# The opening of a four-layer kernel: wider filler products for TensorE, gated loads, another order of the first loads

## The chip, the cores and the metric

The program runs on one core of one Trainium2 chip. A core has a matrix engine (TensorE, "PE" in the profile; its weight loads are "PEld"), three engines for elementwise work (VectorE "DVE", ScalarE "ACT", GpSimd "POOL") and SyncE ("SP"), which here only issues DMAs. The metric is the device time of one execution in microseconds (us). Before the change the median of three runs is 757.54 us, with the runs between 756.88 and 757.93.

## What is computed

`x` has 64 sequences of 64 tokens with 256 features (4096 tokens), and `cond` has one vector of 64 numbers for each sequence. Four layers follow each other:

```python
# layer 0: conditioned RMS norm, GELU-gated FFN, 8-bit activations and ternary weights in the down product
scale = cond @ norm_w.T + 1.0
h = x * (scale[:, None, :] * rsqrt(mean(x * x) + 1e-6))
val, gate = split(h @ up_w.T)                     # 2 x 1024
x = act_quant(val * gelu(gate)) @ weight_quant(down_w).T + x
# layer 1: conditioned RMS norm, attention with 16 heads in each sequence; norm, SwiGLU FFN (1024)
x = x + a_alpha * attention(norm(x)) ; x = x + f_alpha * swiglu(norm(x))
# layer 2: layer norm plus tanh(cond @ lin_w.T + lin_b)
# layer 3: adapter whose two matrices are made from cond for each sequence
Wd_b = Wd + 0.1 * (cond @ Wdd.T + bdd) ; Wu_b = Wu + 0.1 * (cond @ Wdu.T + bdu)
x = x + relu(x @ Wd_b + bd) @ Wu_b + bu
```

The arrays are fp32. The large products take each operand as a high and a low part in a 32-bit matmul format and add up three products of the parts (high-high, high-low, low-high).

## The kernel before

The tokens are worked on in 8 blocks of 512, each block in 4 tiles of 128. Layer 0 is one loop over the 32 tiles (`l0`, with n the tile's number); the change lies in its opening, before tile 2, and in three loads that the loop issues.

**A tile of layer 0.** `upper(n, ch)` makes, for each of two halves `ch` of the 1024 gate and value columns, 12 products of 512 columns into one PSUM bank for the gate and 12 into one for the value (`mm3`, L83 to L85; for tiles 0 and 1 `first`, L423). ScalarE applies GELU to the gate bank (L441), VectorE multiplies with the value bank (L442). `quant(n)` on VectorE rounds the result to whole numbers (L448 to L453), and a transposing DMA on SP turns it round (L455). `lower(n)`, some three tiles later, makes the down product (L467), and VectorE scales it and adds x (L468). The eight PSUM banks go round among all of these. At set tiles ("visits", first n = 5, 9 and 12) four generator blocks for layer 3 are made as well (`gen_make`, L289; `gen_stage`, L304; `gen_store`, L311, which is a DMA issued by POOL).

**Splitting weights.** Weights arrive in fp32 in a staging tile; ScalarE makes the high part by a copy (`half_hi`, L332), VectorE the low part by a subtraction (`half_lo`, L336). The same is done for x times its scale (`prep_parts`, L401 to L406; for the first half block at L497 to L500). For the weights of attention this is the class `Splitter`: `load` (L195) brings one 128x256 piece to one of two staging buffers, `turn` (L201, L202) splits the oldest piece that is there and loads another. The loop calls `load` at tile 7 and `turn` at tiles 8 to 15.

**Who sets the order.** On PE, ACT, DVE and POOL the order is that of the program text. SP's order is that of the text in the opening alone; after it a planner puts SP's DMAs in the order in which it expects them to be able to go, so that a load whose buffer is free early can go out far ahead of its place in the text. Three loads do: the two first pieces of the attention weights (`st`), and block 2's x (`xt`). Where the program must hold a load back, GpSimd writes one column of its target first, reading something that is ready only at the wanted time: the load then has to wait for that write (L278 for the generator's weights, L378 for block 1's x, L387 for `upst3`).

**The opening.** SP issues `condT` (L105), the two chunks of the first half block of x in feature-major form (L374), then `upst3`, x's first block in token-major form (`xt0`, L389), `upst1`, the rest of x's block (L391) and `condT` again (L392). ACT issues the norm's weights (`cwn`, L106) and the four pieces of `upst2` and `upst0` (L328). TensorE meanwhile runs six filler products (`warm`, L477) of a zeroed tile `idle`, the scale's products (`cond_vector`, L121), and five filler products more. Then `first((0, 1), 0)` and `first((0, 1), 1)` make the 48 products of tiles 0 and 1, in the order up2, up0, up3, up1 of the weights. Block 0's sums of squares (`prep_scale`, L223) stand on ACT between the split of up3 and that of up1.

Of the kernel before, what the change touches and what calls it, by code (L numbers as in the profile page):

```python
# [8 lines left out]
F32 = mybir.dt.float32  # L9
F32R = mybir.dt.float32r  # L10
BF16 = mybir.dt.bfloat16
# [6 lines left out]
P = 128  # L18
# [4 lines left out]
T = 512  # L23
# [13 lines left out]
def tile_kernel(ctx: ExitStack, tc, xT, x, condT, cw, upT, downT, qkvT, woT, ghT, outT_w,  # L37
                vecs, rows, g1, g2, gb, out):
    nc = tc.nc

    const = ctx.enter_context(tc.tile_pool(name="const", bufs=1))
# [10 lines left out]
    pools = {}  # L52
# [9 lines left out]
    def bank(tag):  # L62
        uid[0] += 1
        tags = pools["tags"]
        if tag not in tags:
            tag = "mm"
        return pools["ps"].tile([P, 512], F32, tag=tag, bufs=tags[tag], name=f"{tag}_{uid[0]}")
# [6 lines left out]
    def block(name):  # L74
        return main.tile([P, TT, D], F32, tag="x1", bufs=X1, name=name)

    def tok(ap, i):

        return ap[i * T:(i + 1) * T, :].rearrange("(t p) d -> p t d", p=P)
# [16 lines left out]

    ident = const.tile([P, P], F32, name="ident")
    make_identity(nc, ident)
    idle = const.tile([P, P], F32, name="idle")
    nhalf = const.tile([P, TT], F32, name="nhalf")  # L100
    nc.vector.memset(idle, 0.0)
    nc.gpsimd.memset(nhalf, -0.5)
    ct = const.tile([P, NB], F32, name="ct")
    cwn = main.tile([64, D], F32, tag="st", bufs=2, name="cwn")
    nc.sync.dma_start(out=ct[0:64], in_=condT)  # L105
    nc.scalar.dma_start(out=cwn, in_=cw[:, V_NORM, :])  # L106

    gl = pools["a"].tile([P, NB], F32, name="gl")
# [72 lines left out]
    class Splitter:  # L181
# [5 lines left out]
                         for hi, lo, src, kc, n, step in jobs for c in range(kc) for j in range(0, n, step)]  # L187
            self.there = []

        def load(self):  # L190
            if self.todo:
                hi, lo, v, c, js = self.todo.pop(0)
                uid[0] += 1
                st = main.tile([P, 512], F32, tag="st", bufs=2, name=f"st{uid[0]}")[:, :js.stop - js.start]
                nc.sync.dma_start(out=st, in_=v[:, c, js])  # L195
                self.there.append((hi[:, c, js], lo[:, c, js], st))

        def turn(self):
            if self.there:
                hi, lo, st = self.there.pop(0)  # L200
                nc.scalar.copy(hi, st)  # L201
                self.eng.tensor_tensor(lo, st, hi.bitcast(F32), ALU.subtract)  # L202
            self.load()

    def two(pool, name, kc, n):
        return [pool.tile([P, kc, n], F32R, name=f"{name}{k}") for k in range(2)]
# [19 lines left out]
    def parts(name):  # L226
        return [main.tile([P, 2, T], F32R, tag=k, bufs=2, name=f"{k}{name}") for k in ("xh", "xl")]
# [86 lines left out]
    def l0(hooks):  # L314
# [6 lines left out]
        blk, til = {}, {}  # L321

        ups, xfs = {}, {}

        def load_up(j, queue, chunks=slice(0, 2)):
            if j not in ups:
                ups[j] = main.tile([P, 2, 512], F32, tag="x1", bufs=X1, name=f"upst{j}")
            queue.dma_start(out=ups[j][:, chunks],  # L328
                            in_=upT.rearrange("(c p) n -> p c n", p=P)[:, chunks, j * 512:(j + 1) * 512])
# [35 lines left out]
        def prep_load(i):  # L365
            xf = pool.tile([P, 2, T], F32, tag="xf", bufs=1, name=f"xf{i}")
            xt = None if i == 0 else block(f"xt{i}")
            xfs[i] = xf
            blk[i] = [xt, None, parts(f"l0_{i}"), None]
            src = xT.rearrange("(c p) t -> p c t", p=P)[:, :, i * T:(i + 1) * T]  # L370
            if i == 0:

                for c in range(2):
                    nc.sync.dma_start(out=xf[:, c, :T // 2], in_=src[:, c, :T // 2])  # L374
            else:
                nc.sync.dma_start(out=xf, in_=src)
                if i == 1:
                    nc.gpsimd.tensor_copy(xt[:, 0, 0:1], ups[1][:, 0, 0:1])  # L378
                nc.sync.dma_start(out=xt, in_=tok(x, i))

        def rest_load():
# [91 lines left out]
        def warm(n):  # L473

            pb = bank("mm")
            for _ in range(n):
                nc.tensor.matmul(pb[:, :P], lhsT=idle, rhs=idle, start=True, stop=True)  # L477

        for c in range(2):
            load_up(2, nc.scalar, slice(c, c + 1))  # L480
        prep_load(0)
        til["ones"] = pool.tile([P, P], F32, name="ones")

        nc.scalar.activation(sa, nhalf[:, 0:2], AF.Gelu)
        nc.gpsimd.memset(til["ones"], 1.0)
        for c in range(2):
            load_up(0, nc.scalar, slice(c, c + 1))
        rest_load()
        warm(6)
        half_hi(2, 0)  # L490
        cond_norm()
        warm(5)

        for c in range(2):
# [31 lines left out]
        for n in range(N + 2):  # L526
            if n < N:
                if n > 1:
                    upper(n, 0)
                if n == 0:  # L530
                    ternary_load()
                if n in visits:
                    for _ in range(4):
                        gen_make()
                        gen_stage()
                for _ in range(0 if n == 4 else 2 if n in visits and (n + 3 in visits or n == visits[-1]) else 1):
                    gen_load(ups[1][:, n % 2, n:n + 1] if n < 4 else None)
                    gen_store()
                upper(n, 1, "rest" if n < 2 else None)
                if n == 1:  # L540
                    ternary()
                    blk[0][3] = block("x1_0")
                if n == 4:
                    ternary_rest()
                if n % TT == 0 and n // TT + 1 < NBLK:
                    prep_load(n // TT + 1)
                if n % TT == 1 and n // TT + 1 < NBLK:
                    for _ in prep_parts(n // TT + 1):
                        pass
                if n % TT == 2 and n // TT + 1 < NBLK:  # L550
                    prep_scale(n // TT + 1)
# [443 lines left out]
    nc.gpsimd.memset(vx, 0.0)  # L995
    splits = Splitter(nc.vector, (qkv[0], qkv[1], qkvT, 2, 3 * D, 256), (wo[0], wo[1], woT, 2, D, 256))

    hooks = {2: [cond_load], 7: [splits.load]}
    for n in range(8, 16):
        hooks[n] = [splits.turn]  # L1000
    hooks[10].append(cond_rest)
    last = NBLK * TT
    turned = []
# [11 lines left out]
    hooks[last] = [lambda: a_ahead(0, 5), lambda: turned[0](), lambda: turn_ahead(1), lambda: a_ahead(0, 6), lambda: a_ahead(0, 7)]  # L1015
    hooks[last + 1] = [lambda: turned[1](), lambda: a_begin(2)]
    l0(hooks)
    phase.close()

# [8 lines left out]
    splits = Splitter(nc.gpsimd, (*pools["gh"], ghT, 2, 2 * FF, 512), (*pools["wout"], outT_w, 8, D, 256))  # L1028
# [17 lines left out]
    for w in range(W):  # L1046
        i, tp = divmod(w, 2)
# [87 lines left out]
    for n in range(5, N):  # L1135
        i, f = divmod(n, 8)
# [123 lines left out]
```

## Time and profile before

| | us |
|---|---|
| median of three runs | 757.54 |
| profiled execution | 757.83 |
| its span, first to last instruction | 755.9 |
| PE busy in the span | 744.7 |
| DVE busy | 540.9 |
| ACT busy | 405.8 |
| POOL busy | 340.4 |

Matmuls are pipelined and their ends are modelled, so PE's busy share says little; the distance between the starts of neighbouring matmuls says more. A row of the timeline gives start, duration, engine, line, operation, output and inputs, shapes, the number of instructions that are merged in it and, in brackets, how long the engine had been idle and what ended that. "SPq" and "ACTq" rows are DMA issues. A DMA row gives the queue's engine, the size and the median time from issue to landing.

### The profile page before, as it was taken

How to read it: one execution, taken by the hardware profiler on the slowest of the kernel's cores; microseconds unless marked ns; L12 is line 12 of the kernel's file. 1: busy time of each engine (PE TensorE's matmuls, PEld its weight loads, DVE VectorE, ACT ScalarE, POOL GpSimd, SP SyncE). 2: the span in 40 equal slices, each digit the busy share in tenths (PEclk: the TensorE clock that was granted, in tenths of full speed). 3: DMA queues.
4: the chain of work that ended last, by engine and by line, in shares of the span. 5: the costliest groups of instructions: out<-in, count | busy, mean ns of one | idle time of the engine just before them, and what ended most of it. 6: DMA issues, size and time to landing. Idle time of an engine off the chain costs nothing.

```text
span 755.9 us, 17443 instructions
## 1 busy us (share of the span) xinstructions
PE 744.7 (99%) x7036; PEld 616.5 (82%) x7036; DVE 540.9 (72%) x841; ACT 405.8 (54%) x848; POOL 340.4 (45%) x359
## 2 busy tenths in 40 slices
PE   9999999999999999999999999999999999999997
PEld 7866766776676878888888888888888888888886
DVE  4998878867687688889888866636465555555666
ACT  5553445335435588998889573535253534434242
POOL 2123223123134436766655327464646464545291
PEclk9999999999999999999999999999999999999999
DMA  8897999999995866444665237623261708080821
GB/s 241 253 264 166 270 282 222 296 274 260 223 266 115 186 156 167 113 126 120 160 148 127 80 103 183 140 65 76 72 152 45 179 17 208 1 195 2 229 51 57
DMA packets 117457, 118.88 MB, mean 157 GB/s; under 512 B 39633, under 2 KB 101201, under 8 KB 117377
## 3 DMA queue, kind: packets, MB, share of 16 engines
q1 hardware_dynamic: 109232, 91.29, 49.6%
q0 software_dynamic: 7488, 25.37, 10.8%
q10 hardware_dynamic: 656, 1.11, 0.5%
q8 instruction: 55, 0.90, 0.5%
q14 instruction: 26, 0.20, 0.1%
HBM read 71.41 MB, written 29.56 MB: 134 GB/s over the span
## 4 chain that ended last, share of the span: by engine, by line
PE 84%; DVE 7%; ACT 3%; DMA 3%; issue 2%; POOL 1%; SPq 0%; DVEq 0%; ACTq 0%; POOLq 0%
PE mm L83 10%; PE mm L85 9%; PE mm L84 9%; PE gh L83 7%; PE gh L84 7%; PE gh L85 7%; PE acc L83 4%; PE acc L85 4%; PE acc L84 4%; PE mm L467 4%; PE mm L289 4%; PE S L640 2%; DMA rows<-alphad 2%; PE mm L938 2%; PE mm L681 2%
## 5 line engine op out<-in xcount | busy, mean ns | idle before, releaser
L83 PE MATMUL mm<-up,xhl 128*128 128x512 f32 x240 | 98.0, 408 | 0.0
L83 PE MATMUL gh<-xhf,gh 128*128 128x512 f32 x244 | 97.2, 398 | 0.0
L84 PE MATMUL gh<-xlf,gh 128*128 128x512 f32 x244 | 96.9, 397 | 0.0
L85 PE MATMUL gh<-xhf,gh 128*128 128x512 f32 x244 | 96.9, 397 | 0.0
L787 DVE TENSOR_TENSOR sg<-gh,sg 128x512 f32<-128x512 f32 x61 | 42.0, 688 | 76.0 <-ACT sg L786 39.9
L84 PE MATMUL mm<-up,xhl 128*128 128x512 f32 x240 | 94.8, 395 | 0.0
L85 PE MATMUL mm<-up,xll 128*128 128x512 f32 x240 | 94.8, 395 | 0.0
L441 ACT ACTIVATE g<-mm,rs_l 128x512 f32<-128x512 f32 x64 | 43.8, 689 | 82.7 <-PE mm L85 52.0
L815 DVE TENSOR_TENSOR hlo<-sg,hhi 128x512 fp32r<-128x512 f32 x59 | 56.0, 949 | 31.1 <-ACT hhi L814 30.3
L814 ACT CAST hhi<-sg 128x512 fp32r<-128x512 f32 x59 | 36.5, 619 | 74.2 <-DVE sg L787 73.3
L83 PE MATMUL acc<-wout,hhi 128*128 128x256 f32 x248 | 72.7, 293 | 0.0
L85 PE MATMUL acc<-wout,hlo 128*128 128x256 f32 x248 | 70.3, 283 | 1.1 <-DVE hlo L815 1.1
L442 DVE SCALAR_TENSOR_TENSOR h<-mm,rs_l,g 128x512 f32<-128x512 f32 x64 | 46.5, 744 | 34.6 <-PE mm L85 31.2
L84 PE MATMUL acc<-wout,hhi 128*128 128x256 f32 x248 | 70.1, 282 | 0.0
L251 POOL TENSOR_TENSOR xg<-xg,cv 128x512 f32<-128x512 f32 x32 | 35.3, 1113 | 71.4 <-DVE xg L250 67.3
L83 PEld LDWEIGHTS mm<-up,xhl 128*128 128x128 f32 x240 | 45.1, 188 | 16.2 <-issue 2.4
L85 PEld LDWEIGHTS gh<-xhf,gh 128*128 128x128 f32 x244 | 46.1, 189 | 10.8
L85 PEld LDWEIGHTS mm<-up,xll 128*128 128x128 f32 x240 | 45.0, 188 | 11.0
L84 PEld LDWEIGHTS gh<-xlf,gh 128*128 128x128 f32 x244 | 46.3, 190 | 8.1
L83 PEld LDWEIGHTS gh<-xhf,gh 128*128 128x128 f32 x244 | 46.3, 190 | 8.1
L84 PEld LDWEIGHTS mm<-up,xhl 128*128 128x128 f32 x240 | 45.2, 188 | 9.4
L651 DVE TENSOR_REDUCE mx<-S 128x16 f32<-128x1024 f32 x32 | 39.1, 1221 | 17.3 <-PE S L640 17.3
(215 smaller groups left out, 1928.1 us busy)
## 6 DMA issues: line engine op xcount, KB each, us to landing
gt<-in_g SPq DMA_DIRECT2D x32, 512.0 KB, 9.0
rows<-alphad SPq DMA_DIRECT2D x48, 256.0 KB, 5.1
vb<-vx SPq DMA_DIRECT2D x32, 256.0 KB, 5.3
wd<-s1d SPq DMA_DIRECT2D x32, 256.0 KB, 6.4
wu<-s2d SPq DMA_DIRECT2D x32, 256.0 KB, 6.3
xt<-in_x SPq DMA_DIRECT2D x8, 512.0 KB, 8.4
s1d<-stgs POOLq DMA_DIRECT2D x16, 256.0 KB, 7.3
s1d<-stg POOLq DMA_DIRECT2D x16, 256.0 KB, 7.3
```

The lines of the kernel that those rows point to most:

```text
L83: nc.tensor.matmul(out, lhsT=l[0], rhs=r[0], start=first, stop=False)
L84: nc.tensor.matmul(out, lhsT=l[0], rhs=r[1], start=False, stop=False)
L85: nc.tensor.matmul(out, lhsT=l[1], rhs=r[0], start=False, stop=last)
L251: nc.gpsimd.tensor_tensor(b3(xg), b3(xg), bc(vb, c, i), ALU.add)
L289: nc.tensor.matmul(pb[s][c * 64:(c + 1) * 64], lhsT=gl[h], rhs=gt[h, c * GC:(c + 1) * GC], start=True, stop=True, tile_position=(64 * s, 6 ...
L441: nc.scalar.activation(g, pg, AF.Gelu, scale=rs[:, t:t + 1])
L442: nc.vector.scalar_tensor_tensor(h[:, ch * 512:(ch + 1) * 512], pv, rs[:, t:t + 1], g, ALU.mult, ALU.mult)
L467: nc.tensor.matmul(py[:, :D], lhsT=qt[:, f, :], rhs=wq[:, f, :], start=f == 0, stop=f == 7)
L651: nc.vector.tensor_reduce(ms, sv, AX.X, ALU.max)
L787: nc.vector.tensor_tensor(sg, pv, sg, ALU.mult)
L814: nc.scalar.copy(h_hi, sg)
L815: nc.vector.tensor_tensor(h_lo, sg, h_hi.bitcast(F32), ALU.subtract)
```

## The change

There are three parts.

- The filler. `idle` is a bf16 tile of 128x512 in place of an fp32 tile of 128x128, and each filler product multiplies its first 128 columns with all 512. The counts stay six and five.
- The order of the first loads. On SP the first chunk of x goes first and `condT` second. The second chunk of x goes out on ACT's queue between the two pieces of `upst2`.
- Gates. The first two pieces of the attention weights (the `load` at tile 7 and that in the `turn` at tile 8) are held by a GpSimd write from `gl`, and block 2's x is held by a GpSimd write from `xt0`. GpSimd runs these three writes where they stand in the text: that for block 2's x after the gates of tile 3, the first `st` gate after POOL's store of block 0's result and two generator stores, the second after two generator stores more.

```diff
-    idle = const.tile([P, P], F32, name="idle")
+    idle = pools["a"].tile([P, 512], BF16, name="idle")
...
-    nc.sync.dma_start(out=ct[0:64], in_=condT)
     nc.scalar.dma_start(out=cwn, in_=cw[:, V_NORM, :])
...
-        def load(self):
+        def load(self, held=False):
...
+                if held:
+
+                    nc.gpsimd.tensor_copy(st[:, 0:1], gl[:, 0:1])
                 nc.sync.dma_start(out=st, in_=v[:, c, js])
...
-        def turn(self):
+        def turn(self, held=False):
...
-            self.load()
+            self.load(held)
...
-                for c in range(2):
-                    nc.sync.dma_start(out=xf[:, c, :T // 2], in_=src[:, c, :T // 2])
+                nc.sync.dma_start(out=xf[:, 0, :T // 2], in_=src[:, 0, :T // 2])
+                nc.sync.dma_start(out=ct[0:64], in_=condT)
             else:
                 nc.sync.dma_start(out=xf, in_=src)
-                if i == 1:
-                    nc.gpsimd.tensor_copy(xt[:, 0, 0:1], ups[1][:, 0, 0:1])
+                if i < 3:
+                    nc.gpsimd.tensor_copy(xt[:, 0, 0:1], ups[1][:, 0, 0:1] if i == 1 else blk[0][0][:, 0, 0:1])
                 nc.sync.dma_start(out=xt, in_=tok(x, i))
...
-                nc.tensor.matmul(pb[:, :P], lhsT=idle, rhs=idle, start=True, stop=True)
-
-        for c in range(2):
-            load_up(2, nc.scalar, slice(c, c + 1))
+                nc.tensor.matmul(pb, lhsT=idle[:, :P], rhs=idle, start=True, stop=True)
+
+        load_up(2, nc.scalar, slice(0, 1))
         prep_load(0)
...
+        nc.scalar.dma_start(out=xfs[0][:, 1, :T // 2], in_=xT[P:2 * P, :T // 2])
+        load_up(2, nc.scalar, slice(1, 2))
...
-    hooks = {2: [cond_load], 7: [splits.load]}
+    hooks = {2: [cond_load], 7: [lambda: splits.load(True)]}
     for n in range(8, 16):
-        hooks[n] = [splits.turn]
+        hooks[n] = [lambda n=n: splits.turn(n == 8)]
```

## The prediction

> **What bounds the kernel now.** I read the page's table of engines first (PE 744.7 of 755.9 us busy, so any PE delay goes to the end), then the opening in the timeline, then VectorE's waits, then the timeline where the gated loads are used. Lines of the opening:
>
> ```profile
> 1.05 2.93 PE L477 MATMUL mm<-idle 128*128 128x128 f32 x12 [1.05 <-DVE idle L101]
> ...
> 4.95 2.50 PE L477 MATMUL mm<-idle 128*128 128x128 f32 x10
> ...
> 7.10 2.05 PE L423 MATMUL mm<-up,xhl 128*128 128x512 f32 x4
> ...
> 9.60 1.09 PE L423 MATMUL mm<-up,xhl 128*128 128x512 f32 x4
> ...
> 11.56 0.62 ACT L332 CAST up<-upst 128x512 fp32r<-128x512 f32 x1 [3.13 <-DMA upst<-in_upT]
> ...
> 13.85 0.42 ACT L223 ACTIVATE junkl<-xt 128x256 f32<-128x256 f32 x1 [0.25 <-DMA xt<-in_x]
> ...
> 15.89 1.12 ACT L332 CAST up<-upst 128x512 fp32r<-128x512 f32 x2
> ...
> 16.52 1.29 DVE L336 TENSOR_TENSOR up<-upst,up 128x512 fp32r<-128x512 f32 x2 [2.13 <-ACT up L332]
> ```
>
> Four products take 1.85 us at 7.10 (to the start of the next pair at 8.95), 0.46 each, and 0.93 us at 9.60 (to 10.53), 0.23 each: PE runs at half its rate until about 9.4, though the granted clock in the windows from 0 to 21 us reads 1.00. Then loads bind: ACT waits 3.13 us for up0's second piece, then for xt0 until 13.85; its four squares take 2.04 us, and only then up1 is split, at 15.89. At 16.52 VectorE starts, and its waits in the window from 16.6 to 74 us are, whole:
>
> ```profile
> DVE up L336 <- ACT up L332: 2.1, 1, 2.1
> DVE x L468 <- DVE am L464: 0.2, 1, 0.2
> ```
>
> The first is the wait ending at 16.52. From there VectorE works for 57 us without waiting for another engine. So PE and VectorE are two chains side by side. They meet here (the first row of ACT and of DVE is the use of the first attention piece):
>
> ```profile
> 63.51 0.82 POOL L470 DMA_DIRECT2D x1d<-x  x1 [6.03 <-DVE x L468]
> 64.33 1.23 POOL L311 DMA_DIRECT2D s1d<-stgs  x2
> ...
> 66.89 0.39 ACT L201 CAST qkv<-st 128x256 fp32r<-128x256 f32 x1
> ...
> 69.73 0.42 DVE L202 TENSOR_TENSOR qkv<-st,qkv 128x256 fp32r<-128x256 f32 x1
> 69.99 0.69 ACT L441 ACTIVATE g<-mm,rs_l 128x512 f32<-128x512 f32 x1 [2.71 <-PE mm L85]
> ...
> 73.41 0.48 DVE L468 SCALAR_TENSOR_TENSOR x<-mm,am,xt 128x256 f32<-128x256 f32 x1
> 73.81 0.74 DVE L442 SCALAR_TENSOR_TENSOR h<-mm,rs_l,g 128x512 f32<-128x512 f32 x1
> ```
>
> The generator products at 71.29 (L289) start, group by group, in steps of 0.48, 0.43, 0.43, 0.43, 0.43, 0.47: the seventh group, at 73.95, is 0.04 late. It is the one whose product waits for VectorE by the program's order, and VectorE's L468 ends at 73.89. So at tile 9 VectorE's chain has only that slack: 0.04 us before PE stands. After 74.55 VectorE idles 3.59 us, until 78.15; later delays of it are absorbed.
>
> **The change part by part.**
>
> *Filler.* 22 filler instructions of 0.213 us spacing (5.4 us) become 11. At 0.427 us for 512 columns, the start-to-start time of the products at 7.7 to 8.5, six take 2.6 us and five 2.1 us; at 0.233 us the five take 1.2. The memset (0.17 us for 128 columns) takes 0.17 to 0.68 for 512, and lies before the wait for `condT`. Two cases: PE is at full rate by the first product, or again only near 9.4. With full rate the first product starts when its data is there and the first 18 end about 1.4 us earlier than now; then they wait for up0's second piece, as ACT does already. With half rate the filler ends near 7.7 and the first product is 0.6 us later. Before gave full rate 2.3 us after dense 512-column products began, so I take the first case.
> The Trainium skill ("TensorE: Matmul & The Clock Gate", Part 1) says that the full clock comes after some 3.4 us of sustained activity in a free-running window. By that the new filler, from 1.2 us, would bring it between 4.6 and 8.0, and the rate itself would give 1.4 us. The trace speaks against counting that: it stands ahead of loads that bind.
>
> *First loads.* `condT` is issued one DMA later on SP (xf's rows lie 0.64 us after it, so 1.4 for 0.73); its landing takes 2.8 us, so 4.2 for 3.5; cv and the first scaled x come 0.2 to 0.5 us later (now 5.05 and 5.52). The second chunk of x is issued at about 1.95 for 2.23; VectorE wants it 1.3 us after the first, so the second chunk's splits stay where they are. up2's second piece and up0's pieces go out 0.5 us later on ACT's queue; ACT needs up2's at 6.29 and holds 0.6 us in reserve between up0's second piece and xt0 (three casts of 0.52 from 11.56 reach 13.2, xt0 comes at 13.82). No cost taken.
>
> *Gates.* Three GpSimd writes of 0.18 us, on an engine that idles for 10 us at these places: nothing by themselves. Two effects count.
> (a) The first piece of `st` (128 KB, issued at 2.70 ahead of up3 and xt0) leaves the opening. DMA moves 245 to 363 GB/s there, so xt0 lands about 0.4 us earlier (131 kB at 310). The second piece and block 2's x were issued at 8.58 and 12.94, behind xt0. As squares, up1's split and VectorE's chain follow xt0, the gain is 0.4 us. Bounds: 1.0, if the first load's earlier start (0.64) adds to it; -0.2, if PE stays at half rate until 9.4 (0.6 later, less 0.4 that PE loses now to late splits at 12.96, 13.30, 17.61 and 36.78).
> (b) The first gated `st` now goes out late. On POOL its write stands behind block 0's store, 63.51, and two generator stores, which end at 65.56; so 65.56 + 0.18, issue on SP at 65.80 (SP is free then: the next transpose goes at 67.75). ACT wants the piece at 66.89, VectorE its high part at 69.73. What the load takes is the disputed price. Three rows of the same load, each one DMA in a narrow window:
>
> ```profile
> st<-in_qkvT SPq DMA_DIRECT2D x1, 128.0 KB, 2.3
> ...
> st<-in_qkvT SPq DMA_DIRECT2D x1, 128.0 KB, 4.6
> ...
> st<-in_qkvT SPq DMA_DIRECT2D x1, 128.0 KB, 6.0
> ```
>
> 2.3 at 91.26 with the DMA quiet; 4.6 at 96.62, with block 1's store (95.24) and generator stores just issued by POOL; 6.0 at 71.36, behind a transpose and a 512 KB load on its own queue. At 65.80 POOL has issued block 0's store and generator stores, and DMA is 0.94 to 1.01 busy from 65 to 69: nearest is 4.6. Landing 70.4, ACT's cast 70.45 to 70.85 (ACT stands from 66.99; its GELU moves from 69.99 to 70.9 and is used only at 73.81), VectorE's L202 at 70.9 for 69.73: 1.15 late. All behind it on VectorE is late too, L468 among it, and PE's generator group at 73.95 stands 1.1 us. Bounds: 0 (at 2.3, landing 68.1) and 2.5 (at 6.0, landing 71.8).
> The Trainium skill ("DMA: Bandwidth & Descriptors", Queues, rings and completion order) says that each DMA engine goes round between the queues that have work, a packet at a time. By it a small load on SP's queue would not wait for POOL's stores, would land near the quiet 2.3, and cost nothing: 757.1. The row at 96.62 shows otherwise, 4.6 beside such stores, and decides.
>
> The second gated piece goes out behind the 512 KB load, at 71.3, and is used at 80.66: 9.4 us, free even at 6.0. Block 2's x can go after the transpose at 36.28, so from 37.6; ACT squares it at 53.96: 16 us, against 8.7 for the slowest such load. Later delay of `gt` by it: its fourth tile is used 1.8 us after it lands (40.59), so free.
>
> **Sum.** The later of the two chains counts at 73.95: VectorE's comes at -0.4 + 1.1 = +0.7 us, PE's own would come at -0.4 or, at half rate, +0.2. So +0.7 us. The profiled execution of 757.83 (755.9 span and 1.9 around it) becomes 758.5; it lies 0.3 above the median, so the median goes from 757.54 to 758.2. Nothing gives it back: PE starts its products without gaps from 74.97 on. About 0.2% (1.5 us) is what a measurement of this kernel can tell from no change.
>
> **The rivals.**
> 1. *The gated piece lands in time* (within 3.5 us of its issue): the opening's gain stays, 757.1 (756.5 to 757.6). For it: the load is small and the quiet row 2.3. Against: POOL's stores fill the DMA just then. It would need xt0 a full 1.5 us earlier as well to be told from no change.
> 2. *The gated piece is later than I think* and decides: at 6.0 us VectorE is 2.5 late, sum 2.1, 759.6, slower. It decides from 5.4 us on (5.4 - 3.5 - 0.4 = 1.5). For it: the row at 71.36. Against: nothing stands ahead of it on SP's queue.
> 3. *The filler doesn't do what it says*: half rate until about 9.4 again. Then PE's chain comes 0.2 late by itself. With the piece late that hides behind VectorE's +0.7; with the piece in time the sum is +0.2, 757.7. For it: the wait for `condT` gets longer and falls into the filler. Against: 2.3 us of dense products were enough.
>
> **How the numbers follow.** My forecast 0.52 (757.6 to 759.0), rival 1 0.22, rival 2 0.18, rival 3 with the piece in time 0.08. Range: the lower end takes most of rival 1, 756.6; the upper end goes past rival 2's centre, 759.9, short of the worst bounds together (no gain and 2.5, 760.0). Faster by over 0.2% only if xt0 comes much earlier and the piece in time: 0.09. Slower: rival 2 and the upper tail of the forecast, 0.24. The rest, 0.67, is within 0.2%.
>
> **What would show it.** In the changed kernel: spacing of the first products 0.23 in place of 0.43; `xt` squares at about 13.4 for 13.85, and VectorE's chain from about 16.1; the `st` DMA issued near 65.4 with its time to landing; ACT idle before its first L201 cast until the piece lands, VectorE idle before its first L202 by about 1.1 us, and PE late by as much within the generator products near 73.5. It is wrong if L202 shows no wait there, if PE does not stand when VectorE does, or if the opening moves VectorE's start by more than 1.0 us.

## The result and the profile after

Nine runs of the changed kernel have a median of 759.43 us (758.24 to 760.47); nine of the kernel before, beside them, 757.38 (756.88 to 757.93). The ratio is 1.0028, with a 95% interval of 1.0019 to 1.0037: the change makes the kernel slower by 0.28%, some 2.05 us. The forecast was 758.2 (756.6 to 759.9). The measured time lies inside that range and on the forecast side, but the loss is some 2.05 us where 0.7 was forecast, and 759.43 is outside the 757.6 to 759.0 that the prediction gave to its main case.

The profiled execution took 760.47 us, the slowest of the nine, with a span of 758.4; that of before took 757.83, with 755.9. So the two traces differ by 2.5 us of span. Lines after 95 have moved by up to three (L423 of before is L425, L202 is L204, L468 is L470, L289 is L291).

The opening, from the timeline of the changed kernel (start, duration, engine, line, operation; in brackets the idle time before and what ended it):

```profile
1.17 0.57 SPq L376 DMA_DIRECT2D ct<-in_condT  x1
...
1.18 2.74 PE L479 MATMUL mm<-idle 128*128 128x512 bf16 x6 [1.18 <-DVE idle L101]
...
5.30 1.09 PE L120 MATMUL mm<-ct,cwn 64*128 64x64 f32 x4 [1.38 <-DMA ct<-in_condT]
...
8.07 2.27 PE L425 MATMUL mm<-up,xhl 128*128 128x512 f32 x4
...
12.67 1.09 PE L425 MATMUL mm<-up,xhl 128*128 128x512 f32 x4
...
13.32 0.42 ACT L225 ACTIVATE junkl<-xt 128x256 f32<-128x256 f32 x1
...
16.01 1.29 DVE L338 TENSOR_TENSOR up<-upst,up 128x512 fp32r<-128x512 f32 x2 [1.81 <-ACT up L334]
...
21.07 0.40 PE L83 MATMUL mm<-up,xhl 128*128 128x512 f32 x1
...
21.11 0.75 DVE L444 SCALAR_TENSOR_TENSOR h<-mm,rs_l,g 128x512 f32<-128x512 f32 x1 [1.04 <-PE mm L425]
```

Rows of before to set beside it, those that the prediction does not show:

```profile
3.90 1.11 PE L121 MATMUL mm<-ct,cwn 64*128 64x64 f32 x4
...
19.70 0.40 PE L83 MATMUL mm<-up,xhl 128*128 128x512 f32 x1
...
20.50 0.74 DVE L442 SCALAR_TENSOR_TENSOR h<-mm,rs_l,g 128x512 f32<-128x512 f32 x1
```

The DMA row of `condT`, first before and then changed:

```profile
ct<-in_condT SPq DMA_DIRECT2D x1, 16.0 KB, 2.8
...
ct<-in_condT SPq DMA_DIRECT2D x1, 16.0 KB, 4.0
```

`condT` is issued 0.44 us later than before and needs 4.0 us to land (5.17) instead of 2.8 (3.50). TensorE's six wide products are through by 3.92, so it stands 1.38 us, and its first real product starts at 8.07 for 7.10. Full rate (0.23 us from product to product) comes at 11.74 for 9.37, and the 48 products of the opening end at 21.07 for 19.70: 1.37 us late. The gain on the other chain is there: xt0's squares start at 13.32 for 13.85, VectorE's splits at 16.01 for 16.52, 0.51 us early. The waits of VectorE in the window from 16 to 74 us show where that goes (total, times, longest):

```profile
DVE up L338 <- ACT up L334: 1.8, 1, 1.8
DVE qkv L204 <- ACT qkv L203: 1.3, 1, 1.3
DVE h L444 <- PE mm L425: 1.0, 1, 1.0
DVE x L470 <- DVE am L466: 0.2, 1, 0.2
```

Two rows are new. At 21.11 VectorE waits 1.04 us for the late TensorE, which turns 0.51 early into 0.6 late (21.11 for 20.50); and it waits 1.28 us for the gated piece. That place, tile 9, in the timeline:

```profile
64.08 0.82 POOL L472 DMA_DIRECT2D x1d<-x  x1 [4.59 <-DVE x L470]
...
66.13 0.20 POOL L196 COPY st<-gl 128x1 f32<-128x1 f32 x1
...
66.35 0.33 SPq L197 DMA_DIRECT2D st<-in_qkvT  x1
...
71.23 0.41 ACT L203 CAST qkv<-st 128x256 fp32r<-128x256 f32 x1 [3.04 <-DMA st<-in_qkvT]
...
71.67 0.43 DVE L204 TENSOR_TENSOR qkv<-st,qkv 128x256 fp32r<-128x256 f32 x1 [1.28 <-ACT qkv L203]
...
75.35 0.48 DVE L470 SCALAR_TENSOR_TENSOR x<-mm,am,xt 128x256 f32<-128x256 f32 x1
...
75.89 1.09 PE L291 MATMUL mm<-gt,gl 64*64 64x512 f32 x8 [0.60 <-DVE x L470]
...
76.91 0.50 PE L83 MATMUL mm<-up,xhl 128*128 128x512 f32 x1
```

The gate stands behind POOL's stores, so the load is issued at 66.35; it lands at 71.15, 4.80 us later. ScalarE, VectorE and at last TensorE wait: its seventh generator group at 75.89 comes 1.19 us after the sixth, where a group takes 0.41, so it stands 0.78. VectorE's L470 is at 75.35 for 73.41, and TensorE's first product behind the generators at 76.91 for 74.97: 1.94 us late. From there the shift stays near 1.9 for some 220 us, and VectorE's last instruction is 1.73 us late. The other 0.75 us of the span's 2.5 lies behind that instruction, where SP's last six DMA issues take 3.98 us for 3.25; the second trace of the changed kernel (e9 below) has 1.79 and 0.26 there. The second gated piece and block 2's x, issued late as well, let nobody wait.

### The profile page after: what moved, and what is told of

The parts are those of the page before. It is cut to its first block, busy times and chain, and to the rows that moved or that the text cites. A ratio compares the mean times of both kernels' runs of the same rounds, so it can differ in the third digit from the quotient of the medians.

```text
span 758.4 us, 17430 instructions
## 1 busy us (share of the span) xinstructions
PE 744.5 (98%) x7025; PEld 613.8 (81%) x7025; DVE 541.0 (71%) x841; ACT 406.2 (54%) x848; POOL 342.1 (45%) x362
## 4 chain that ended last, share of the span: by engine, by line
PE 81%; DVE 7%; ACT 5%; DMA 3%; issue 2%; SPq 1%; POOL 1%; DVEq 0%; ACTq 0%; POOLq 0%
PE mm L83 9%; PE mm L85 9%; PE mm L84 9%; PE gh L83 7%; PE gh L84 7%; PE gh L85 7%; PE acc L83 4%; PE acc L85 4%; PE acc L84 4%; PE mm L469 4%; PE mm L291 4%; PE mm L941 2%; PE S L643 2%; DMA rows<-alphad 2%; PE mm L684 2%
## 5 line engine op out<-in xcount | busy, mean ns | idle before, releaser
L789 ACT ACTIVATE sg<-gh 128x512 f32<-128x512 f32 x61 | 35.9, 589 | 29.0 <-PE gh L85 28.4
```

The lines of the kernel that those rows point to most:

```text
L789: nc.scalar.activation(sg, pg, AF.Silu)
```

## The experiments

The theory has two parts. *The gate*: the first gated piece lands too late, and TensorE stands at tile 9. *The first loads*: `condT` is late, TensorE's dense products begin later, and it arrives late at tile 9 by itself. The rival to the first is that the whole loss comes from the opening; the rival to the second, that the order of the loads costs nothing (as predicted) and the wide filler is at fault, or chance. The kernels undo one part of the change or add one part to the kernel before.

This table is read from the profiled execution of each (us from the span's start): the landing of `condT`, the first real product, the start of full rate among the real products, the end of the 48 products of the opening, VectorE's wait before its first split of a piece of `st`, and TensorE's first product behind tile 9's generator products, here "next product". The ratio is that of times to the kernel before beside it, with its 95% interval; it is not simply the quotient of the two medians (for e1 that would be 1.0023).

| kernel | condT | first | full rate | 48 end | wait | next product | ratio |
|---|---|---|---|---|---|---|---|
| before | 3.50 | 7.10 | 9.37 | 19.70 | 0.00 | 74.97 | 1 |
| changed | 5.17 | 8.07 | 11.74 | 21.07 | 1.28 | 76.91 | 1.0028 (1.0019 to 1.0037) |
| changed, again (e9) | 5.08 | 7.99 | 12.11 | 21.21 | 1.17 | 76.92 | 1.0033 (1.0022 to 1.0044) |
| changed without gates on `st` (e1) | 4.33 | 7.23 | 9.66 | 19.68 | 0.00 | 74.69 | 1.0012 (0.9997 to 1.0027) |
| the same again (e10) | 4.54 | 7.03 | 7.37 | 18.47 | 0.00 | 73.47 | 1.0012 (1.0001 to 1.0024) |
| changed, first piece called at tile 4 (e2) | 4.70 | 6.74 | 7.08 | 19.95 | 0.00 | 75.16 | 1.0010 (0.9998 to 1.0023) |
| changed with the old order (e5) | 3.22 | 6.77 | 9.86 | 19.42 | 1.06 | 75.02 | 1.0012 (1.0002 to 1.0022) |
| changed with more filler (e8) | 4.98 | 7.24 | 7.58 | 19.11 | 1.06 | 75.47 | 1.0020 (1.0010 to 1.0030) |
| before plus gates on `st` (e3) | 3.28 | 7.10 | 10.52 | 19.84 | 1.16 | 75.58 | 1.0014 (1.0003 to 1.0025) |
| before plus new order (e4) | 5.34 | 7.38 | 11.13 | 20.23 | 0.00 | 75.25 | 1.0007 (0.9995 to 1.0020) |
| before plus wide filler (e6) | 3.25 | 6.65 | 10.31 | 19.65 | 0.00 | 74.66 | 1.0008 (0.9998 to 1.0018) |
| old order, wide filler, piece at tile 4 (e7) | 3.31 | 6.94 | 8.66 | 18.99 | 0.00 | 74.19 | 1.0002 (0.9993 to 1.0011) |
| before plus gates, piece at tile 4 (e12) | 3.30 | 7.10 | 10.10 | 19.66 | 0.00 | 74.67 | 1.0003 (0.9992 to 1.0014) |
| before plus gates, piece later still (e11) | 3.80 | 7.10 | 9.68 | 19.46 | 5.83 | 81.48 | 1.0121 (1.0103 to 1.0139) |

Single executions scatter: the 28 to 35 runs of before beside the experiments lie between 755.86 and 760.32. Below, one trace shows a mechanism, and the ratio says what it is worth.

### A. The gates on `st` taken out of the changed kernel

```diff
-    hooks = {2: [cond_load], 7: [lambda: splits.load(True)]}
+    hooks = {2: [cond_load], 7: [splits.load]}
     for n in range(8, 16):
-        hooks[n] = [lambda n=n: splits.turn(n == 8)]
+        hooks[n] = [splits.turn]
```

> The changed kernel with the two gates of the attention pieces (st) taken out; filler, new order of the first loads and the gate of block 2's x stay. Late-piece theory: VectorE's 1.28 us wait before its first L204 and the 0.78 us that PE stands in the generator products at 75.9 vanish, so about 1.3 us less than the changed kernel: 758.1. Opening theory (all of the loss comes from the later condT, whose wait on PE grew to 1.38 us, and from PE's half rate until 11.6): the time stays near 759.4. Both expect PE's first half-rate products and the late end of the 48 first products (21.07) to stay.

759.09 us against 757.37, a median 1.7 above, while the ratio, 1.0012 (0.9997 to 1.0027), leaves open whether it is slower at all: its twelve runs reach from 755.47 to 761.03. The trace is clear where the time isn't: no wait at tile 9, groups of generator products in steps of 0.41 and 0.46. So it was run once more, with the changed kernel beside it.

> The changed kernel once more, to have it beside the same runs of the kernel before as the next ones. Both theories: 1.5 to 2.7 us over the kernel before. Trace: VectorE's wait at the first qkv split 1.0 to 1.4 us whatever the opening does; condT at 4.3 to 5.4, full rate anywhere between 7 and 12.

> The first experiment again (the changed kernel without the gates of the attention pieces), beside the changed kernel itself, since its twelve times spread over 5.6 us. Late-piece theory: 0.8 to 1.3 us below the changed kernel of this call. Opening theory: equal to it.

On one chip: changed kernel 759.41 (ratio 1.0033), without the gates 757.92 (1.0012), before 757.14. The gates on `st` cost some 1.5 us in the changed kernel by these medians; e1's ratio makes it 1.2. The same place in the timeline of the kernel without them:

```profile
65.48 0.40 ACT L203 CAST qkv<-st 128x256 fp32r<-128x256 f32 x1
...
68.24 0.42 DVE L204 TENSOR_TENSOR qkv<-st,qkv 128x256 fp32r<-128x256 f32 x1
69.88 0.21 PEld L291 LDWEIGHTS mm<-gt,gl 64*64 64x64 f32 x8 [0.36 <-issue]
69.88 3.66 PE L291 MATMUL mm<-gt,gl 64*64 64x512 f32 x32
```

ScalarE and VectorE show no brackets, and all 32 generator products stand in one row without a gap.

One thing that both theories expected failed: the late end of the 48 products did not stay at 21.07 but came at 19.68 (e1) and 18.47 (e10), with the new order in place. So these two traces differ from that of the changed kernel by more than the wait at tile 9, and the price of the gates is read from the times.

Nor was xt0 later for having the piece in the opening. Its squares start at 13.12 in e1 and here, in e10, at 12.22, for 13.32 (changed) and 13.63 (e9) with the gates:

```profile
12.22 0.42 ACT L225 ACTIVATE junkl<-xt 128x256 f32<-128x256 f32 x1 [0.28 <-DMA xt<-in_x]
```

### B. The gates on `st` alone, in the kernel before

```diff
+                if held:
+                    nc.gpsimd.tensor_copy(st[:, 0:1], gl[:, 0:1])
                 nc.sync.dma_start(out=st, in_=v[:, c, js])
...
-    hooks = {2: [cond_load], 7: [splits.load]}
+    hooks = {2: [cond_load], 7: [lambda: splits.load(True)]}
...
-        hooks[n] = [splits.turn]
+        hooks[n] = [lambda n=n: splits.turn(n == 8)]
```

> The kernel before with the two st gates alone; old filler, old order, block 2's x not gated. Late-piece theory: the opening gains about 0.4 us (xt0 lands near 13.4), VectorE waits 1.2 us at its first qkv split and PE about 0.8 to 1.1 in the generator products: 0.7 over the kernel before, 758.1. Opening theory: the gates cost nothing, 757.0 to 757.4.

758.15 us, ratio 1.0014 (1.0003 to 1.0025): slower by about 1.1 us by the ratio, 0.8 by the medians. The load goes out at 65.15 and takes 4.7 us. Its waits of VectorE, same view and window as above:

```profile
DVE qkv L204 <- ACT qkv L203: 1.2, 1, 1.2
DVE h L444 <- PE mm L425: 0.8, 1, 0.8
DVE x L470 <- DVE am L466: 0.2, 1, 0.2
```

The wait is there with nothing else changed, and TensorE's longest step among the generators is 1.08 for 0.41.

### C. The piece in time, everything else as changed

```diff
-    hooks = {2: [cond_load], 7: [lambda: splits.load(True)]}
+    hooks = {2: [cond_load], 4: [lambda: splits.load(True)]}
```

> The changed kernel with the first gated st load called at tile 4 in place of tile 7, so that GpSimd's gate stands ahead of its stores and not behind them; everything else as changed. It keeps the opening free of the piece. Late-piece theory: the load goes out near 38 us, no wait at L204, 758.1 (as without gates, or 0.1 to 0.4 less if the opening without the piece counts). Opening theory: 759.4.

757.99 us, ratio 1.0010 (0.9998 to 1.0023). The load is issued at 39.10 and lands at 45.44: no wait. This execution reached full rate at 4.5, inside the wait for `condT`, and yet its 48 products ended at 19.95, no earlier than before. Its timeline says why:

```profile
9.65 1.09 PE L425 MATMUL mm<-up,xhl 128*128 128x512 f32 x4
10.58 0.63 PE L425 MATMUL mm<-up,xll 128*128 128x512 f32 x2
12.29 0.50 PE L425 MATMUL mm<-up,xhl 128*128 128x512 f32 x1 [1.08 <-ACT up L334]
```

After 18 products TensorE waits 1.08 us for up0's second piece: loads bind, as the prediction held against counting the rate as a gain.

### D. The old order, the new order alone, and the wide filler alone

The first of these puts `condT` first and both chunks of x on SP again in the changed kernel; the second has the new order and nothing else, the third the filler and nothing else.

```diff
+    nc.sync.dma_start(out=ct[0:64], in_=condT)
     nc.scalar.dma_start(out=cwn, in_=cw[:, V_NORM, :])
...
-                nc.sync.dma_start(out=xf[:, 0, :T // 2], in_=src[:, 0, :T // 2])
-                nc.sync.dma_start(out=ct[0:64], in_=condT)
+                for c in range(2):
+                    nc.sync.dma_start(out=xf[:, c, :T // 2], in_=src[:, c, :T // 2])
...
-        load_up(2, nc.scalar, slice(0, 1))
+        for c in range(2):
+            load_up(2, nc.scalar, slice(c, c + 1))
...
-        nc.scalar.dma_start(out=xfs[0][:, 1, :T // 2], in_=xT[P:2 * P, :T // 2])
-        load_up(2, nc.scalar, slice(1, 2))
```

> The changed kernel with the old order of the first loads (condT first, both chunks of x on SP); the wide filler and all gates stay. Opening theory, now with numbers from the traces (condT landed at 4.3 to 5.3 with the new order, at 3.3 to 3.5 with the old; PE came to its full rate at 9.7 to 11.7 against 9.4 to 10.5): condT near 3.5, no wait on PE before its products, full rate by 9.4 or earlier. Late-piece theory: VectorE still waits 1.2 us at its first qkv split and a generator step of PE is 0.7 to 0.8 us long. Together 758.1 to 758.6. If the two causes do not add up, 757.4.

758.31 us, ratio 1.0012 (1.0002 to 1.0022). `condT` lands at 3.22, the 48 products end at 19.42 instead of 21.07, while VectorE's wait at tile 9 is still there (1.06). So the wait at tile 9 does not need the new order. That TensorE's late opening does is less plain: the seven traces with the new order end the 48 products between 18.47 and 21.21, the seven with the old one between 18.99 and 19.84. The latest three (21.21 and 21.07 in the changed kernel, 20.23 in e4) have the new order, but e1, e2, e8 and e10 have it too and end at 18.47 to 19.95; the section on the hardware says what else has to come in. Full rate came at 9.86, not by 9.4 as expected.

```diff
-    nc.sync.dma_start(out=ct[0:64], in_=condT)
...
-                for c in range(2):
-                    nc.sync.dma_start(out=xf[:, c, :T // 2], in_=src[:, c, :T // 2])
+                nc.sync.dma_start(out=xf[:, 0, :T // 2], in_=src[:, 0, :T // 2])
+                nc.sync.dma_start(out=ct[0:64], in_=condT)
...
+        nc.scalar.dma_start(out=xfs[0][:, 1, :T // 2], in_=xT[P:2 * P, :T // 2])
+        load_up(2, nc.scalar, slice(1, 2))
```

> The kernel before with the new order of the first loads alone (x's first chunk ahead of condT on SP, the second chunk on ACT's queue between up2's pieces). Late-piece theory with my recorded step (condT 0.7 us later, hidden behind the loads): 757.4. Opening theory: condT lands near 5.2 for 3.5, PE waits for it and stays at half rate until after 11: 0.6 to 1.2 over the kernel before, 758.0 to 758.6.

758.00 us, ratio 1.0007 (0.9995 to 1.0020): not told from no change. The trace shows the later `condT` by itself: `condT` lands at 5.34, TensorE stands 1.50 us before the scale's products, and the 48 products end at 20.23, 0.53 late.

```diff
-    idle = const.tile([P, P], F32, name="idle")
+    idle = pools["a"].tile([P, 512], BF16, name="idle")
...
-                nc.tensor.matmul(pb[:, :P], lhsT=idle, rhs=idle, start=True, stop=True)
+                nc.tensor.matmul(pb, lhsT=idle[:, :P], rhs=idle, start=True, stop=True)
```

> The kernel before with the wide filler alone. If dense 512-column products bring PE's full rate sooner: full rate before the first real product (spacing 0.23 from it on) and the 48 first products end 0.2 to 0.5 us earlier, 757.0 to 757.4, since loads bind. If the filler is no better than the old one for the rate: full rate at 9.4 or later, the first product near 7.4, 757.4 to 757.8.

757.69 us, ratio 1.0008 (0.9998 to 1.0018). Full rate came at 10.31, where before had 9.37: the wide filler alone does not bring it earlier.

### E. Filler until `condT` is there

```diff
-        warm(6)
+        warm(11)
```

> The changed kernel with eleven wide filler products in place of six ahead of condT's products, so that PE has no gap there (6 x 0.43 us end near 3.8, 11 near 5.9, condT lands at 4.3 to 5.3). If it is the gap that keeps the rate at half: full rate by 8 us, first products 0.23 apart, the 48 end 0.5 to 1.0 us earlier than the changed kernel's 21.07; the late piece stays: 758.1 to 758.8. If the rate comes at a time that the filler does not set: full rate between 9 and 12 as before, 759.4 to 760.

758.76 us, ratio 1.0020 (1.0010 to 1.0030). Full rate came inside the filler, at 4.55; TensorE ended its 48 products at 19.11, 1.96 us before the changed kernel and more than the expected 0.5 to 1.0, and reached the generators at 70.53, 0.76 us ahead of before. There it lost the lead:

```profile
70.22 0.43 DVE L204 TENSOR_TENSOR qkv<-st,qkv 128x256 fp32r<-128x256 f32 x1 [1.06 <-ACT qkv L203]
...
70.53 2.81 PE L291 MATMUL mm<-gt,gl 64*64 64x512 f32 x24
...
74.45 1.09 PE L291 MATMUL mm<-gt,gl 64*64 64x512 f32 x8 [1.12 <-DVE x L470]
```

Its step to the seventh group is 1.71, so it stands 1.30, more than in the changed kernel (0.78), because it came earlier and VectorE did not. The later of the two chains counts.

### F. The gate moved later still

```diff
-    hooks = {2: [cond_load], 7: [splits.load]}
+    hooks = {2: [cond_load], 7: [lambda: nc.gpsimd.memset(vx[:, 0:1], 0.0), lambda: splits.load(True)]}
```

This is the kernel of B with one more small GpSimd write of zeros ahead of the gate, on a tile that is zero already; with it the planner puts the load behind the next transpose on SP. The expectation speaks of 512 columns of zeros; the kernel that ran writes one.

> The kernel before with the two st gates, and a GpSimd write of 128x512 zeros ahead of the first gate, into a tile that is still all zeros. The planner then puts the first gated load behind the next transpose on SP: issue near 70.2 in place of 65.2, landing 74 to 76. Late-piece theory: VectorE waits 5 to 6.5 us at its first qkv split and PE stands 4.5 to 6 us in the generator products: 4 to 5.5 us more than with the gates alone, 761.5 to 763.5. If VectorE's later idle time (3.59 us at 78.15) took up such a wait: at most 760.

766.49 us, ratio 1.0121 (1.0103 to 1.0139). The piece is issued at 70.43 for 65.15 and takes 4.4 us; VectorE waits 5.83. The direction is as expected, the size is not: 9 us instead of some 4 to 6. The next product comes 6.5 us late, and behind it more is lost:

```profile
74.90 0.40 ACT L203 CAST qkv<-st 128x256 fp32r<-128x256 f32 x1 [8.18 <-DMA st<-in_qkvT]
...
75.34 0.43 DVE L204 TENSOR_TENSOR qkv<-st,qkv 128x256 fp32r<-128x256 f32 x1 [5.83 <-ACT qkv L203]
...
75.95 1.08 PE L291 MATMUL mm<-gt,gl 64*64 64x512 f32 x6 [2.14 <-ACT g L443]
...
79.56 1.99 PE L291 MATMUL mm<-gt,gl 64*64 64x512 f32 x8 [2.53 <-DVE x L470]
```

TensorE stands twice: until 75.95 for ScalarE's GELU, which is queued behind the cast, and until 79.56 for VectorE's L470, each time some 3 us behind the product before (2.73 and 3.12). Then its clock falls. Stretches of this trace, with the busy time (and number) of PE, PEld, DVE, ACT and POOL, the granted clock, the DMA's share and GB/s:

```profile
70.94:74.36 3.42, 2.87 (x19) 0.78 (x18) 0.00 (x0) 0.00 (x0) 0.00 (x0) 1.00 1.06 157
74.36:77.77 3.41, 1.08 (x6) 0.20 (x6) 2.33 (x5) 2.87 (x7) 0.62 (x1) 1.00 0.70 226
77.77:81.19 3.42, 1.63 (x8) 0.31 (x8) 2.26 (x5) 1.04 (x3) 3.42 (x6) 0.50 0.70 129
81.19:84.60 3.41, 3.41 (x11) 2.48 (x8) 0.00 (x0) 1.23 (x3) 0.10 (x1) 0.50 1.03 147
84.60:88.01 3.41, 3.41 (x20) 2.67 (x19) 1.95 (x3) 1.10 (x2) 0.00 (x0) 1.00 1.06 344
```

From 77.77 to 84.60 the granted clock is 0.50, and products of 512 columns follow each other in 0.427 us. From 81.48 on, where TensorE works without a gap, seven of them cost 0.2 us more each, 1.4 us; the last two groups of generator products before them, from 79.56 to 81.48, took 1.92 for the 1.02 of the changed kernel, 0.9 more. That makes 2.3 us, and VectorE's shift agrees: 5.6 us at the piece, 7.9 at its first instruction behind, 7.8 at its last. So a stand has a second price from some length on, which the expectation had left out. The traced execution is the shortest of the four (765.51, 7.7 above the traced one of before); what makes the median 1 us more was not followed up.

### G. The gates in time, with the old order

```diff
-    hooks = {2: [cond_load], 7: [lambda: splits.load(True)]}
+    hooks = {2: [cond_load], 4: [lambda: splits.load(True)]}
```

Beside this line the first of the two has the old order of D with the wide filler, the second the old order and the old filler. Both keep the gate on block 2's x.

> Old order of the first loads, wide filler, block 2's x gated, the first gated st load called at tile 4. Late-piece theory: no wait at the first qkv split, and the opening keeps the room that the pieces leave: 756.9 to 757.4. If the gates cost by themselves, 758.

> The kernel before with the gates alone and the first gated piece called at tile 4; old filler, old order, block 2's x gated. Late-piece theory: no wait at the first qkv split, xt0 0.4 us or more earlier, 756.6 to 757.3, the best of all. If the gates cost by themselves: 757.8 to 758.3.

757.45 us, ratio 1.0002 (0.9993 to 1.0011), and 757.74, ratio 1.0003 (0.9992 to 1.0014). The expectation for the second, the best of all at 756.6 to 757.3, failed. Their traces lie where the gains were hoped for (xt0's squares at 13.13 and 12.24 for 13.85, VectorE's splits at 15.80 and 14.92 for 16.52, the next product at 74.19 and 74.67 for 74.97), 0.3 to 0.8 us, which is less than these times can tell from nothing, and no more than xt0 scatters among the traces. No kernel of the study is measurably faster than the one before.

## Why the prediction was right in direction and short in size

- **The late piece: right in place and size.** Every kernel whose gate stands behind POOL's stores (changed, e3, e5, e8, e9) shows the wait before the split, 1.06 to 1.28 us, and e11, where the load goes later still, 5.83; every kernel without such a gate shows 0.00. Predicted were 4.6 us from issue to landing, 1.15 of wait and a stand of 1.1; the changed kernel has 4.80, 1.28 and 0.78. The stand is shorter because TensorE itself reaches the generators 1.19 us late (72.48 for 71.29). The loads in the other four took 4.6 to 4.7. The row taken from the trace of before, that of a piece issued beside such stores, was the right one, and rival 2 with 6.0 us did not happen. What makes the load slow is not shown: called at tile 4 it took 5.8 to 6.3 us (e2, e7, e12). The Trainium skill ("DMA: Bandwidth & Descriptors", Queues, rings and completion order) says that each DMA engine goes round between its queues a packet at a time. That such a load would land near 2.3 us was the prediction's own inference; that section gives no time for it, and none of the first pieces behind such a gate took less than 4.4.
- **xt0 earlier: the number came, the cause is not shown.** Predicted were 0.4 us for VectorE's start, measured 0.51. But with the new order xt0's squares start at 12.22 to 13.12 in the three traces that load the piece in the opening (e1, e4, e10) and at 13.25 to 14.09 in the four that hold it back (changed, e2, e8, e9), so there the gate did not bring xt0 forward. With the old order they start at 13.49 and 13.85 with the piece and at 12.24 to 13.57 without. The -0.4 of the sum was met by luck, as far as these traces go.
- **"The later of the two chains counts at tile 9": right,** and shown by e8, where TensorE lost its lead.
- **The first loads, "No cost taken": the step that failed.** The working gave `condT` the 2.8 us to land that it took when it was first on its queue. Second, it took 4.0 in the changed kernel; over the seven traces with the new order it landed between 4.33 and 5.34, over the seven with the old one between 3.22 and 3.80. So the scale's products start up to 1.6 us later (5.48 in e4, 5.30 in the changed kernel, 3.90 before). Whether the 48 products then end late depends on when full rate comes (D); in both traces of the changed kernel they do, by 1.37 and 1.51 us.
- **The filler: the wrong case was taken.** I took full rate by the first product, since before had it 2.3 us after its dense products began. That interval is not fixed: e11, e12 and e3, which also begin them at 7.10, have it 2.6, 3.0 and 3.4 us after. Rival 3 happened instead, and worse than I priced it: not "near 9.4 again" but 11.74, of which 0.97 us is that the dense products begin later. The filler's length was also misread: 22 products 0.213 us apart make 4.7 us; 5.4 is what their two rows last. Nothing hung on that.
- **The sum.** VectorE's chain was to come 0.4 early and 1.1 late, +0.7, and TensorE's at +0.2 at worst. In fact TensorE ended the opening 1.37 late in the trace, and by it VectorE waited 1.04 us at 21.11 (0.89 in e9). With VectorE's own terms: -0.51 + 1.04 + 1.28 = +1.8, against 1.94 found at L470. The term that is missing is the 1.04. It also made the load later: block 0's store waits for VectorE's x, so the load went out at 66.35 and not near 65.4. That the total falls near the number of rival 2 (759.6) is a coincidence of another cause.
- **"Nothing gives it back": not quite.** What a trace is late or early at tile 9 against before holds to about 300 us and then changes: from about 80 us to VectorE's last instruction e3 goes from +0.61 to +0.24, e8 from +0.48 to -0.21, e4 from +0.29 to -0.54, the changed kernel from +1.93 to +1.73. What gives it back there was not followed up.

How the loss divides in time: the gates alone give +0.14%, the order alone +0.07%, the filler alone +0.08%, the last two with intervals that include zero; together 0.29%, against 0.28% found. That they add up so well is more than their intervals can bear; the gates' share is the part that is shown from both sides (A and B). The order's share is not shown to the same degree: its late `condT` is in every trace, and e5's ratio of 1.0012 stands against 1.0028 and 1.0033 for the changed kernel, but alone (e4) it cannot be told from nothing. The gate on block 2's x was not tried alone; in the changed kernel's trace nobody waits for it.

Open is why `condT` takes longer as the second load on its queue, 3.1 to 4.2 us for 2.5 to 3.1; that was not tried. Nor was filler up to `condT` tried together with a piece in time, which might keep TensorE's lead of e8.

## What the runs showed of the hardware

**The rate comes at the end of a fixed stretch of 3.41 us, if TensorE was busy enough in it.** The granted clock read 1.00 for the opening of before, in which products plainly ran at half rate. The reason is that the trace's records of the clock begin only with the first change: at 9.35 us in before (0.23 us spacing from 9.37), at 11.61 in the changed kernel (11.74), and so in all fourteen traces, within 0.2 us where products of 512 columns follow to show it. Where no record stands, the view prints 1.00. One trace, that of the new order alone (e4), has the rise, the fall and the rise again (columns as in F):

```profile
4.11:7.52 3.41, 2.04 (x15) 1.85 (x16) 1.35 (x4) 1.22 (x3) 0.00 (x0) 1.00 0.92 309
7.52:10.93 3.41, 3.41 (x9) 2.63 (x10) 2.29 (x5) 1.73 (x4) 0.00 (x0) 0.50 1.00 325
```

It rose at 4.11, and from 4.11 to 7.52, with 2.04 of 3.41 us busy because `condT` was late, it lost the rate again; full rate came at 10.93. The lengths of all records but the last in each trace are whole multiples of 3.413 us (in e11: 68.267, 6.827 and 679.252, that is 20, 2 and 199). Where the first stretch begins relative to the program differs from execution to execution: the rises lie at 4.11 to 4.55 in four traces and at 8.48 to 12.02 in the other ten.

Counted from the products' rows over these stretches, backwards from the rise, and leaving out the scale's four small products (64 rows, 64 columns), a stretch that raised the rate had TensorE busy for 0.80 or more of it, and no stretch with 0.75 or less did (the ends of the rows are modelled, so these shares are rough). The small ones cannot count in full: in before the stretch from 2.53 to 5.94 is full with them and 0.71 without, and the rate did not rise. Six wide products last 2.74 us, 0.80 of a stretch, twelve narrow ones 2.93, 0.86: both can raise the rate only if the stretch happens to hold nearly all of them, as in e2, e10 and e4. Otherwise the rate must wait for a stretch behind the scale's products, whose end the late `condT` moves from 4.95 to 6.32. With eleven (e8) the stretch was 0.99 full. This account fits all fourteen traces: it has the wide filler no better than the narrow one, and a late `condT` bringing the rate later unless the first filler has already raised it. It was worked out from these traces afterwards, and only e8 changes the filler's length on purpose. Whether this chance is what scatters the times of one kernel is not shown, and one pair of traces speaks against it: e1 and e10, the same kernel, have their rises at 9.57 and 4.41 and their next products 1.22 us apart, and yet spans of 754.87 and 754.92.

To keep the rate a stretch may be emptier than to raise it. In e2 the one from 11.33 to 14.75 was busy for 2.46 us (0.72) and in e10 the one from 4.41 to 7.82 for 2.60 (0.76, or 0.60 without the small products), and the rate stayed; it fell after 2.04 us (e4) and 1.08 us (e11).

The Trainium skill ("TensorE: Matmul & The Clock Gate", Part 1) describes this as a free-running window of 3413 ns; the records agree. Its table lets the clock fall after an idle window; here it fell after windows that were busy for 2.04 (e4) and 1.08 us (e11) of 3.41. My prediction used the page for a time of onset, 4.6 to 8.0; none of the fourteen first rises lies there. By the count above, the pause behind the filler and the small products left the stretches in between too empty.

## What to carry to other kernels

A gate keeps a load out of a crowded stretch, but the load then starts when the gate's own engine reaches it: look at what stands ahead of the gate in that engine's order (here DMA issues), add the time that such a load takes beside the traffic of that moment, and compare with its first use; called three tiles earlier, the same gate let nobody wait. To have TensorE at full rate in an opening, count the share of each 3.41 us in which dense products run, from the first product to the first real one, and close the gap before the first load that they depend on (one trace, e8), before making the products wider. Put the load that ends TensorE's first wait first on its queue: second, it landed here at 4.33 to 5.34 us, first, at 3.22 to 3.80. And check a gain that came as forecast against a kernel that lacks its supposed cause: xt0 was early without the gates as well.
